# A two-layer graph network on one core: the statistics of a turn ahead of the copies on ScalarE, and folded weights spread over turns 0 to 2

## The chip, the core and the metric

The kernel runs on one core of a Trainium2 chip. The metric is the device time of one execution in microseconds (us); lower is better. The profile's engines are PE (TensorE, the matrix engine), DVE (VectorE), ACT (ScalarE), POOL (GpSimd) and SP (SyncE, which here only issues DMAs). Each engine works through its own queue in order, and waits for the others through semaphores.

## What is computed

The input is `x` (4096 nodes, 512 features) and an adjacency matrix `adj` (4096 x 4096, int32) with about 8 neighbours and the node itself in a row. Two layers are applied, each on a normalized and rectified copy of its input, and each adds its result to the input:

```python
def _L0_gnn_ref(x, adj, WQ, WK, WV, we, be):
    Q = (x @ WQ.T).reshape(n, HEADS, HEAD_DIM).transpose(1, 0, 2)
    ...
    energy = Q @ we.T + be
    attn = jnp.einsum('hqd,hkd->hqk', Q, K) * SCALING + energy
    attn = attn + jnp.where(adj > 0, 0.0, -jnp.inf)
    attn = jax.nn.softmax(attn, axis=-1)
    hard = (attn == jnp.max(attn, axis=-1, keepdims=True)).astype(jnp.float32) / HEADS
    out = jnp.einsum('hqk,hkd->hqd', hard, V)
    return out.transpose(1, 0, 2).reshape(n, EMBED)

def _L1_gnn_ref(x, adj, W_self, b_self, W_nb, b_nb, W_comb, b_comb):
    mask = (adj > 0).astype(x.dtype)
    deg = jnp.sum(mask, axis=1, keepdims=True)
    agg = mask @ x / jnp.maximum(deg, 1.0)
    self_f = x @ W_self + b_self
    nb_f = agg @ W_nb + b_nb
    combined = jnp.concatenate([self_f, nb_f], axis=-1)
    out = combined @ W_comb + b_comb
    return jax.nn.relu(out)

h = jnp.maximum(_layernorm(x, axis=-1), 0.0)
x = x + _L0_gnn_ref(h, adj, ...)
h = jnp.maximum(_layernorm(x, axis=-1), 0.0)
x = x + _L1_gnn_ref(h, adj, ...)
```

Layer 0 is an attention in which each of 8 heads takes the value of the one neighbour with the highest score. Layer 1 sums over the neighbours. `W_comb` is linear, so the kernel multiplies `W_self` and `W_nb` by its two halves once; that is what "fold" means below.

## The kernel before, in words

The work lies in `sparse_path`; `general_path` is compiled behind a flag and does not run on these inputs. There are 32 tiles of 128 nodes, and three phases.

**First phase (0 to about 330 us).** The adjacency is read and packed into words, every node's list of neighbours is found, keys and values are computed and written to `K_d` in DRAM, and the nodes are ranked by degree, so that the tiles are of falling degree. `CAPS` holds the number of list places for each tile (24 for tile 0, 5 for tile 31). What is left over of the value products (`late_v`) is done at the start of the next phase.

**Second phase (about 330 to 985 us).** A loop over turns `i` from -5 to 31 (line 1523). `turns` gives the tile of each turn: tiles 0 to 4 first, then alternately a tile of the lower half (turns 5, 7, 9, ... 27: "fused", whose key and value rows are fetched together) and one of the upper half (turns 6, 8, ... 26: "apart", whose eight winning values are fetched later, head by head), and three fused tiles last. The order of all instructions is written out by hand: each engine's queue has exactly the order of the Python code. One turn issues, in this order:

- on GpSimd, indirect DMAs: the key rows of this turn's tile (`key_gathers`), between them the values of an earlier tile (`value_gathers`), the row of the tile five turns ahead (`rows`), and near the turn's end the scatter of finished layer 1 rows into `G_d` (`scatter`, through `put_rows`, line 1119). The scatter reads `gs`. All gathers have line 1103.
- on ScalarE: `layer1_move` (line 1366, copies the neighbour product `pg` from PSUM to `gs`), `query_copy` (line 1173, `hqT`, for the tile two turns ahead), `layer1_copy` (line 1347, `hT1`), in fused turns the copy of the tile's own values `o` (line 1214), `layer1_stats` (lines 1302 to 1305), `query_norm` (lines 1159 to 1162, for the tile four turns ahead), copies of folded weights (line 1404), and later, after VectorE's reciprocal, `layer1_norm` (lines 1325 to 1329).
- on VectorE: `xo` (line 1288, the layer's sum for a tile of an earlier turn, first half of `layer1_stats`, with its store to `X1_d` on SP's queue), then `scores` (a product, line 1224, and a sum, line 1227, for each group of up to four list places). After the second group come `layer1_inverse` (line 1318, the reciprocal that needs the statistics) and `layer1_out` (line 1372, which reads `gs` and the self product `pr`). `winners` ends the turn: a few small instructions in an apart tile, and in a fused tile seven or eight `copy_predicated` (line 1260) as well.
- on TensorE: the query product of the next turn (line 628, `q`; PSUM holds two of them, so it waits until VectorE has read the last but one), folds, the layer 1 products (`pg` at line 628, `pr` at lines 1358 and 1360; both read `hT1`), the late value products in turns -2 to 0, and two sets of transposes (line 1138).

A dictionary `plan` says in which turn each tile has its steps. Statistics come in turns 3 to 31, one tile a turn up to turn 27 and two in turns 28 and 29; `hT1` and the layer 1 products from turn 5; the move and the scatter from turn 6.

**The folds.** `fold(k, i)` is four matmuls into one of three PSUM buffers and, for `i < 4`, a copy to a quarter of `wN` (k = 1) or `wS` (k = 0) on ScalarE. `i = 4` is the bias; its two products stay in PSUM until `fold_bias` adds them to `bb` on VectorE. `wS` takes the place of the value weights, which the late value products read up to turn 0. The fold's inputs lie in `room`, in which fused turns later put their gathered rows (from turn 5).

**Third phase (about 985 us to the end).** Rows of `G_d` are gathered and summed on VectorE, the widest eight tiles are summed as dense products on TensorE, and the result goes out.

The plan of folds and the part of the loop that is touched:

```python
between = {
    1: [(1, i) for i in range(NC)], 2: [(0, i) for i in range(NC)],
    3: [(1, NC), (0, NC)],
}
...
late(layer1_move, "move", i)
on(query_copy, i + 2)
late(layer1_copy, "layer1", i)
...
late(layer1_stats, "stats", i)
on(query_norm, i + 4)
on(query, i + 1)
for part in between.get(i, ()):
    fold(*part)
late(layer1, "layer1", i)
```

Of the kernel before, what the change touches and what calls it, by code (L numbers as in the profile page):

```python
# [20 lines left out]
NC = D // P  # L21
# [516 lines left out]
def sparse_path(  # L538
# [6 lines left out]
    KT = N // P  # L545
# [62 lines left out]
    def load_fold(k):  # L608
        nc.sync.dma_start(
            F[:, ds(2 * k * NC, NC), :],  # L610
            (wselfT, wnbT)[k].rearrange("(c p) f -> p c f", p=P),
        )
        nc.sync.dma_start(
            F[:, ds((2 * k + 1) * NC, NC), :],
            wcomb[ts(k, D), :].rearrange("(c p) f -> p c f", p=P),
        )
# [9 lines left out]
    def project(dst, h, w):  # L626
        for c in range(NC):
            nc.tensor.matmul(dst, h[:, c, :], w[:, c, :], start=(c == 0), stop=(c == NC - 1))  # L628

    with ExitStack() as pa:  # L630
# [195 lines left out]
        def values(t, ps):  # L826
            pv = ps.tile([P, D], F32, tag="pm", name="pv")
            project(pv, hT(t), ws["wv"])
            return pv

        def values_out(t, pv, pool, eng, vs=None):
            if vs is None:
                vs = pool.tile([P, D], F32, tag="gs", name="vs")

            nc.scalar.activation(vs, pv, AF.Copy, scale=1.0 / H)
            return eng.dma_start(K_d[ts(t, P), 0:D], vs)
# [93 lines left out]
        def on(step, t, *args):  # L930
            if 0 <= t < KT:
                step(t, *args)
# [159 lines left out]
    with ExitStack() as pb:  # L1092
# [9 lines left out]
        def gather(dst, src, idx, at=0):  # L1102
            last[0] = nc.gpsimd.indirect_dma_start(  # L1103
                out=dst, out_offset=None, in_=src,
                in_offset=bass.IndirectOffsetOnAxis(ap=idx, axis=0), element_offset=at,
            )
            if at:

                beyond.append(last[0])
                for w in written:  # L1110
                    tc.declare_no_dep(last[0].ins, w.ins, reason="other columns")
# [97 lines left out]
        def own_values(r):  # L1209

            s = st[r]
            s["o"] = xp.tile([P, D], F32, tag="o", name="o", bufs=3)
            if r in wide:
                nc.scalar.copy(s["o"], s["own"][:, 0:D])
            else:
                gather(s["o"], K_d[:, :], perm[:, r : r + 1])

        def scores(r, within):

            s = st[r]  # L1220
            sc = bp.tile([P, LIST, H], F32, tag="sc", name="sc", bufs=1)
            for kk, g0, g in s["kg"]:
                pr = bp.tile([P, GRP, D], F32, tag="pr", name="pr", bufs=1)
                nc.vector.tensor_tensor(  # L1224
                    pr[:, :g, :], s["q"].unsqueeze(1).to_broadcast([P, g, D]), kk, ALU.mult
                )
                nc.vector.tensor_reduce(  # L1227
                    sc[:, g0 : g0 + g, :],
                    pr[:, :g, :].rearrange("p g (h d) -> p g h d", h=H), AX.X, ALU.add,
                )  # L1230
                if g0:
                    within()
                    within = lambda: None
            s["sc"] = sc
# [148 lines left out]
        def load_bias():  # L1383
            for k in range(2):
                fb = bp.tile([P, D], F32, tag="own", name="fb")
                for c in range(NC):
                    nc.vector.tensor_copy(
                        fb[:, ts(c, P)], bcs[k][:, c : c + 1].to_broadcast([P, P])
                    )
                fbs.append(fb)  # L1390
# [4 lines left out]
        def fold(k, i):  # L1395

            pm = psm.tile([P, D], F32, tag="pm", name="pmw")
            if i < NC:
                left = F[:, ds(2 * k * NC, NC), ts(i, P)]
            else:  # L1400
                left = fbs[k].rearrange("p (c q) -> p c q", q=P)
            project(pm, left, F[:, ds((2 * k + 1) * NC, NC), :])
            if i < NC:
                nc.scalar.copy((wS, wN)[k][:, i, :], pm)
            else:
                biased.append(pm)

        def fold_bias():
            for pm in biased:
                nc.vector.tensor_tensor(bb, pm, bb, ALU.add)  # L1410

        between = {
            1: [(1, i) for i in range(NC)], 2: [(0, i) for i in range(NC)],
            3: [(1, NC), (0, NC)],
        }

        def dense_words():

            wg = gp.tile([P, DENSE, SEG], F32, tag="kg", name="wg")
            for r in range(DENSE):  # L1420
                gather(wg[:, r, :], W_d[:, :], perm[:, r : r + 1])
            return wg
# [50 lines left out]
        i = 0  # L1473
# [20 lines left out]
        def late(step, kind, i, *args):  # L1494

            out_ = []
            for r in turns:
                if plan[kind].get(r) == i:
                    out_ += step(r, *args) or []
            return out_  # L1500

        def tail_turn(r):

            k = tail.index(r)
            at = HALF_R + TAIL0 + k * D
            st[r]["hT1"] = room[:, at : at + D].rearrange("p (c q) -> p c q", q=P)
            nc.scalar.copy(st[r]["hT1"], st[r]["hnp"])

        def tail_product(r):
            s = st[r]  # L1510
            s["pg"] = psm.tile([P, D], F32, tag="pm", name="pg")
            project(s["pg"], s["hT1"], wN)

        def tail_move(r):
            s = st[r]
            s["gs"] = gsl[tail.index(r) // GRP][:, tail.index(r) % GRP]
            nc.scalar.copy(s["gs"], s["pg"])
            put_rows(G_d[:, :], r, s["gs"])
# [4 lines left out]
        for i in range(-5, KT):  # L1523


            if i == -3:
                load_fold(0)
            if i == 0:
                load_bias()
            if i == 1:  # L1530
                wS = wp.tile([P, NC, D], F32, tag="w_b", name="swS")
                wN = bp.tile([P, NC, D], F32, tag="swN", name="swN", bufs=1)
            a, b = on(key_gathers, i), late(value_gathers, "value", i)
            while a or b:
                for q, n in ((a, max(1, round(len(a) / max(1, len(b))))), (b, 1)):
                    for g in q[:n]:
                        gather(*g)
                    del q[:n]
            on(rows, i + 5)
            late(layer1_move, "move", i)  # L1540
            on(query_copy, i + 2)
            late(layer1_copy, "layer1", i)
            early = [r for r in tail if plan["turn"][r] == i - 1]
            for r in early:
                tail_turn(r)
            if i >= 0 and turns[i] in fused:
                own_values(turns[i])
            late(layer1_stats, "stats", i)
            on(query_norm, i + 4)
            on(query, i + 1)  # L1550
            for part in between.get(i, ()):
                fold(*part)
            late(layer1, "layer1", i)
            for r in early:
                tail_product(r)
            if i in (-2, -1, 0):
                n = 2
                for t in late_v[:n]:
                    w = values_out(t, values(t, psm), bp, nc.sync)
                    for g in beyond:  # L1560
                        tc.declare_no_dep(w.ins, g.ins, reason="other columns")
                    written.append(w)
                del late_v[:n]
            if i == max(between) + 1:
                fold_bias()

            def within():
                late(layer1_inverse, "stats", i)
                late(layer1_out, "move", i)

            if i >= 0:
                scores(turns[i], within)
            late(scatter, "move", i)
            if i == KT - 2:
                wg = dense_words()
                gsl = [gp.tile([P, GRP, D], F32, tag="kg", name="gs") for _ in range(2)]
            on(winners, i)
            late(layer1_norm, "stats", i)
            on(query_turn, i + 3)
            late(layer1_turn, "turn", i)  # L1580
            for r in early:
                tail_move(r)
# [161 lines left out]
def kernel(tc, *args):  # L1744
    left = sparse_path(tc, *args)
    with tc.If(left > 0):
        general_path(tc, *args)
# [40 lines left out]
```

## Time and profile before

| what | value |
|---|---|
| six executions, us | 1294.35, 1295.65, 1291.0, 1292.02, 1289.19, 1293.26 |
| their median, us | 1292.64 |
| the profiled execution, us | 1291.67 |
| its span, from first to last instruction, us | 1289.9 |
| PE busy | 1023.0 us (79%) |
| DVE busy | 989.1 us (77%) |
| POOL busy | 775.7 us (60%) |
| ACT busy | 427.6 us (33%) |
| granted TensorE clock, mean | 0.901 |

The busy shares are means over three unlike phases, so they don't say which engine ends which turn. The rows of single instructions do: each has its start, its duration, engine, line, what it writes and reads, how many were merged into the row, and in square brackets the time for which its engine stood idle before it, with what released it. "issue" stands for idle time in which the engine waited for nothing that the profile shows. An indirect DMA on POOL is busy only while GpSimd writes its descriptors; the data land some us later.

The page's slices (busy tenths of the engines in 40 equal parts of the span, 32 us each) show the second phase as slices 11 to 30:

```
DVE  5557777798289776889998889888782479788776
ACT  4778676731221222343434334443531000000000
POOL 2322323233477777777777777777554747777774
```

### The profile page before, as it was taken

What the parts mean: (1) busy time and instruction counts of PE and PEld (TensorE: products, weight loads), DVE (VectorE), ACT (ScalarE), POOL (GpSimd) and SP (SyncE); (2) the same over time, 40 slices, a digit from 0 to 9 for tenths busy, and PEclk for the clock granted to TensorE, in tenths of its full rate; (3) what the DMA queues carried; (4) which work ended last, traced back from release to release, by engine and by line L of the source; (5) the groups of instructions that cost most, each with busy time, mean ns of one, the idle gap of its engine ahead of it and who ended that gap; (6) DMA issues with size and microseconds to landing.
All of it is one profiled execution on the core that took longest, in us unless ns stands there. A gap on an engine that the chain in (4) does not pass through costs nothing.

```text
span 1289.9 us, 10765 instructions
## 1 busy us (share of the span) xinstructions
PE 1023.0 (79%) x2918; PEld 482.5 (37%) x2918; DVE 989.1 (77%) x1650; ACT 427.6 (33%) x880; POOL 775.7 (60%) x910
## 2 busy tenths in 40 slices
PE   5998998948779547757877887888789599999960
PEld 2555555524334223323333333333334244444420
DVE  5557777798289776889998889888782479788776
ACT  4778676731221222343434334443531000000000
POOL 2322323233477777777777777777554747777774
PEclk9999998978899868887889998988899799999985
DMA  9999999749585568888888888887754998888873
GB/s 358 420 420 421 418 420 328 260 147 373 192 255 166 155 187 237 272 272 257 264 264 258 252 249 262 264 246 240 276 179 130 314 347 273 282 272 272 283 248 122
DMA packets 109222, 350.09 MB, mean 271 GB/s; under 512 B 18064, under 2 KB 18064, under 8 KB 100960
## 3 DMA queue, kind: packets, MB, share of 16 engines
q0 software_dynamic: 63376, 208.23, 51.1%
q1 hardware_dynamic: 39552, 129.78, 26.0%
q10 hardware_dynamic: 6224, 11.31, 2.5%
q8 instruction: 25, 0.41, 0.1%
q14 instruction: 45, 0.37, 0.1%
HBM read 285.25 MB, written 68.19 MB: 274 GB/s over the span
## 4 chain that ended last, share of the span: by engine, by line
DMA 16%; POOL 15%; DVE 12%; issue 10%; PE 1%; ACT 1%; DVEq 0%; POOLq 0%
POOL room L1103 10%; DMA room<-G_d,sidx 6%; DMA room<-K_d,sidx 6%; DVE pr L1224 4%; DMA kg<-K_d,sidx 2%; POOL kg L1103 2%; DVE sc L1227 2%; DVE acc L1682 2%; POOL o L1103 2%; DVE o L1260 1%; PE pg L628 1%; DMA o<-K_d,perm 1%; DMA out_dram<-x,perm 1%; POOL out_dram L1119 1%; DVE x L1672 1%
## 5 line engine op out<-in xcount | busy, mean ns | idle before, releaser
L628 PE MATMUL q<-wq,hqT 128*128 128x512 f32 x256 | 160.4, 785 | 144.1 <-DVE pr L1224 144.1
L1660 PE MATMUL da<-gk,mk 128*128 128x512 f32 x512 | 222.5, 598 | 15.4 <-DMA gk<-G_d 15.4
L1103 POOL DMA_INDIRECT room<-G_d,sidx x174 | 179.2, 1030 | 57.7 <-issue 49.4
L1103 POOL DMA_INDIRECT kg<-K_d,sidx x177 | 170.9, 965 | 57.3 <-issue 45.3
L1227 DVE TENSOR_REDUCE sc<-pr 128x32 f32<-128x2048 f32 (+3 forms) x114 | 183.3, 1608 | 3.9
L1682 DVE TENSOR_REDUCE acc<-room 128x512 f32<-128x4096 f32 (+5 forms) x23 | 152.5, 6632 | 14.0 <-DMA room<-G_d,sidx 14.0
L1660 PEld LDWEIGHTS da<-gk,mk 128*128 128x128 f32 x512 | 98.2, 192 | 139.7 <-issue 139.5
L1103 POOL DMA_INDIRECT o<-K_d,vi x128 | 122.3, 955 | 39.0 <-issue 36.9
L628 PEld LDWEIGHTS q<-wq,hqT 128*128 128x128 f32 x256 | 61.8, 253 | 222.7 <-DVE pr L1224 125.7
L628 PE MATMUL pk<-wk,room 128*128 128x512 f32 x256 | 120.7, 616 | 4.2 <-ACT room L810 4.1
L628 PE MATMUL pv<-wv,room 128*128 128x512 f32 x256 | 116.3, 606 | 0.0
L1103 POOL DMA_INDIRECT room<-K_d,sidx x102 | 97.5, 955 | 31.1 <-issue 19.8
L1224 DVE TENSOR_TENSOR pr<-q,kg 128x2048 f32<-128x2048 f32 (+3 forms) x51 | 102.4, 2008 | 15.9 <-DMA kg<-K_d,sidx 14.6
L1224 DVE TENSOR_TENSOR pr<-q,room 128x2048 f32<-128x2048 f32 (+3 forms) x42 | 66.7, 1589 | 55.0 <-DMA room<-K_d,sidx 46.6
L1360 PE MATMUL pr<-swS,hT 128*128 128x512 f32 x216 | 99.9, 605 | 0.0
L628 PE MATMUL pg<-swN,hT 128*128 128x512 f32 x216 | 97.1, 592 | 0.0
L1302 ACT ACTIVATE hn<-xo 128x512 f32<-128x512 f32 x31 | 19.5, 629 | 196.5 <-DVE xo L1288 189.4
L749 ACT ACTIVATE mkt<-adjt,sgb 128x2048 bf16<-128x2048 int32 x37 | 74.2, 2005 | 12.3 <-POOL adjt L670 11.9
L824 POOL DMA_DIRECT2D K_d<-ks x32 | 18.7, 585 | 98.5 <-DVE ks L819 96.3
L1260 DVE COPY_PREDICATED o<-best,room 128x512 f32<-128x512 int32 x102 | 74.5, 730 | 3.5
L628 PEld LDWEIGHTS pv<-wv,room 128*128 128x128 f32 x256 | 49.8, 196 | 61.6 <-issue 61.4
L628 PEld LDWEIGHTS pk<-wk,room 128*128 128x128 f32 x256 | 48.3, 199 | 55.3 <-issue 48.9
(222 smaller groups left out, 1492.9 us busy)
## 6 DMA issues: line engine op xcount, KB each, us to landing
adjt<-adj_dram SPq DMA_DIRECT2D x37, 1024.0 KB, 12.2
room<-adj_dram SPq DMA_DIRECT2D x27, 1024.0 KB, 12.6
x<-X_d SPq DMA_DIRECT2D x32, 512.0 KB, 6.2
xt<-x_dram SPq DMA_DIRECT2D x32, 256.0 KB, 8.6
K_d<-ks POOLq DMA_DIRECT2D x32, 256.0 KB, 6.4
X_d<-xo SPq DMA_DIRECT2D x32, 256.0 KB, 4.2
X_d<-own SPq DMA_DIRECT2D x32, 256.0 KB, 4.8
gk<-G_d ACTq DMA_DIRECT2D x16, 512.0 KB, 5.8
```

The source lines that it names most:

```text
L628: nc.tensor.matmul(dst, h[:, c, :], w[:, c, :], start=(c == 0), stop=(c == NC - 1))
L749: nc.scalar.activation(mk, st[t]["adj"][j], AF.Sigmoid, bias=sgb, scale=400.0, accum_out=degs[:, t, j : j + 1],)
L824: nc.gpsimd.dma_start(K_d[ts(t, P), D : 2 * D], ks)
L1103: last[0] = nc.gpsimd.indirect_dma_start(out=dst, out_offset=None, in_=src, in_offset=bass.IndirectOffsetOnAxis(ap=idx, axis=0), element_o ...
L1119: new = nc.gpsimd.indirect_dma_start(out=dst, out_offset=bass.IndirectOffsetOnAxis(ap=perm[:, r : r + 1], axis=0), in_=src, in_offset=None,)
L1224: nc.vector.tensor_tensor(pr[:, :g, :], s["q"].unsqueeze(1).to_broadcast([P, g, D]), kk, ALU.mult)
L1227: nc.vector.tensor_reduce(sc[:, g0 : g0 + g, :], pr[:, :g, :].rearrange("p g (h d) -> p g h d", h=H), AX.X, ALU.add,)
L1260: nc.vector.copy_predicated(s["o"].rearrange("p (h d) -> p h d", h=H), best[:, k, :].bitcast(I32).unsqueeze(2).to_broadcast([P, H, HD]), b ...
L1302: nc.scalar.activation(junk, xo, AF.Copy, scale=-1.0 / D, accum_out=q[:, 0:1])
L1360: nc.tensor.matmul(pr, s["hT1"][:, c, :], wS[:, c, :], start=False, stop=(c == NC - 1))
L1660: nc.tensor.matmul(dacc[r], masks[s][:, h, r, :], keys[s][:, h, :], start=(s == 0 and h == 0), stop=(s == NPL - 1 and h == 1),)
L1682: nc.vector.tensor_reduce(acc, g[:, 0:n, :].rearrange("p n f -> p f n"), AX.X, ALU.add)
```

## The change

Three things are moved; no instruction is added or taken away.

1. In turns before 28 (`KT - 4`), `layer1_stats` (with its `xo`) is issued ahead of `layer1_move`, `query_copy`, `layer1_copy` and the own values, rather than behind them. From turn 28 on it stays where it was.
2. The eight folds of the weights are issued in turns 0, 1 and 2, as three, three and two, rather than four in turn 1 and four in turn 2. The two bias products stay in turn 3. `wN` is therefore set up in turn 0, `wS` still in turn 1.
3. `fold_bias`, in turn 4, is issued right behind the folds, ahead of the layer 1 products.

```diff
         between = {
-            1: [(1, i) for i in range(NC)], 2: [(0, i) for i in range(NC)],
+            0: [(1, 0), (1, 1), (1, 2)], 1: [(1, 3), (0, 0), (0, 1)], 2: [(0, 2), (0, 3)],
             3: [(1, NC), (0, NC)],
         }
...
             if i == 1:
                 wS = wp.tile([P, NC, D], F32, tag="w_b", name="swS")
+            if i == 0:
+                wS = None
                 wN = bp.tile([P, NC, D], F32, tag="swN", name="swN", bufs=1)
...
             on(rows, i + 5)
+            if i < KT - 4:
+                late(layer1_stats, "stats", i)
             late(layer1_move, "move", i)
             on(query_copy, i + 2)
             late(layer1_copy, "layer1", i)
...
                 own_values(turns[i])
-            late(layer1_stats, "stats", i)
+            if i >= KT - 4:
+                late(layer1_stats, "stats", i)
             on(query_norm, i + 4)
             on(query, i + 1)
             for part in between.get(i, ()):
                 fold(*part)
+            if i == max(between) + 1:
+                fold_bias()
             late(layer1, "layer1", i)
...
-            if i == max(between) + 1:
-                fold_bias()
```

## The prediction

> **What bounds the kernel now.** I first looked at the slices of the page, to see which stretch the edits touch, then at the busy time of each engine in that stretch, then at what GpSimd and VectorE wait for there, and last at the order of time around single turns. The edits touch turns 0 to 27, which in the trace run from 360 to 900 us. The table of stretches (busy us and instructions of each engine) has this for most of it:
>
> ```profile
> core 0: us, PE busy (x) PEld busy (x) DVE busy (x) ACT busy (x) POOL busy (x), PEclk, DMA share, GB/s
> ...
> 396.00:934.00 538.00, 402.45 (x973) 176.43 (x972) 456.53 (x552) 191.62 (x495) 402.96 (x419) 0.87 0.79 243
> ```
>
> GpSimd looks free a quarter of the time, and is not. Its rows there, nearly all gathers, take 0.95 us with 0.30 us before each, whatever released them. 419 rows of 1.25 us are 524 of the 538 us, and most of the rest is one idle time of 8.47 us at the window's end (934.79): up to there no hole is left. VectorE (457 us) does wait; its waits in the same window:
>
> ```profile
> DVE pr L1224 <- DMA room<-K_d,sidx: 41.4, 16, 5.8
> DVE pr L1224 <- DMA kg<-K_d,sidx: 14.6, 8, 4.0
> DVE pr L1224 <- issue: 8.3, 2, 5.8
> DVE q L1318 <- ACT q L1304: 4.2, 1, 4.2
> ```
>
> So in turns 3 to 28 VectorE is late because gathers land late, and they land late because GpSimd issues one after another. The second thing to see is how little the wait that the change aims at weighs: the reciprocal (line 1318) waits for ScalarE's statistics once, 4.2 us at 929.87, in turn 29, and turns from 28 on keep their order.
>
> Now the place of the copies, at the border of turns 9 and 10 (start, us, engine, line). ScalarE:
>
> ```profile
> 577.29 0.59 ACT L1347 COPY hT<-tr 128x512 f32<-128x512 f32 x1
> 591.08 0.63 ACT L1302 ACTIVATE hn<-xo 128x512 f32<-128x512 f32 x1 [13.19 <-DVE xo L1288]
> ...
> 592.88 0.28 ACT L1305 ACTIVATE q<-q,c 128x1 f32<-128x1 f32 x1
> 593.07 0.19 ACT L1159 CAST sidx<-km 128x24 int32<-128x24 f32 x1
> ```
>
> GpSimd at the same time:
>
> ```profile
> 590.18 0.95 POOL L1103 DMA_INDIRECT room<-K_d,perm  x1 [0.31 <-issue]
> 591.43 0.99 POOL L1119 DMA_INDIRECT G_d<-gs,perm  x1 [0.30 <-DMA kg<-K_d,sidx]
> 592.73 0.96 POOL L1103 DMA_INDIRECT room<-K_d,sidx  x1 [0.31 <-DVE sc L1227]
> ```
>
> The three copies of turn 10 were over by 578, and ScalarE then stood 13.19 us in front of the statistics, because `xo` follows VectorE's winners of turn 9. The scatter of turn 10 (line 1119) reads `gs`, the first of those copies, and sits in GpSimd's queue ahead of all gathers of turn 11.
>
> **The change, part by part.** (1) *Statistics first, turns 3 to 27.* The instructions are the same; `xo` and its store on SP's queue keep their place among VectorE's. What is new is a wait: behind the statistics on ScalarE now stand the move to `gs`, the query copy, `hT1` and, in odd turns, the own values. Who waits for each:
>
> - The gain: no wait of the reciprocal lies in these turns, so 0. ScalarE was idle before each of these statistics (25 waits for `xo`, 185.7 us): the copies never held them up.
> - `hT1` is wanted by TensorE's layer 1 products. It comes at the statistics' start S + 1.99 (591.08 to 593.07) and three copies at a pitch of 0.5: S + 3.6. In turn 10 that is 594.7, while the query product ended at 586.2: TensorE gets a hole of 8.5 us. The products' results are read in the next turn: `gs` at the next S + 2, the self product by line 1372 at about the next S + 6, and S to S is 14 to 25 us. With 8.4 us of products (3.60 + 1.12 + 3.70) and 1.0 of transposes TensorE is done at S + 13, and the query product after it, 3.6 us, is wanted a whole turn later. Cost 0; if the hole makes the products cold, see below, still 0.
> - The query copy serves a product issued a turn later, the own values (0.64) winners some 10 us later: 0.
> - `gs`, wanted by the scatter: here the cover is thin. The scatter can't start before S + 1.99, plus the copy's 0.56, plus 0.28 from its end to GpSimd's start (in turn 30 the copy ends at 934.51, the scatter that waits for it starts at 934.79): S + 2.83. I set that against the scatter's present start in each turn. Odd turns have 2.6 to 8.3 us to spare. Even turns, from 6 to 26: -0.13 (512.86 against 510.16 + 2.83), 1.35, **-2.48** (591.43 against 591.08 + 2.83), 0.81, 1.44, 0.78, 0.78, -0.10 (771.33 against 768.60 + 2.83), 3.30, 2.04, 2.04.
>
> In three turns the scatter becomes late, by 0.13 + 2.48 + 0.10 = 2.7 us, with every gather behind it. GpSimd has no hole to make that good in, and VectorE waits for gathers in each odd turn (turn 13: 0.26 and 2.28), so the whole rest shifts: after turn 10 the scatter and S move together, and the later margins stay. At 934.79 GpSimd does idle, 8.47 us, but for a copy that itself hangs on VectorE; no cover there either.
>
> Bounds: the latency that I read once, and the landing of the last gather before each border (5.0 us from issue to use in turn 7, 6.3 in turn 9), move all margins. One us better leaves 1.5 us (turn 10 alone). One us worse gives 1.13 + 3.48 + 0.19 + 0.22 + 0.22 + 1.10 = 6.3. A lost margin costs while a gained one gives nothing, so I take a quarter us to the worse side: 0.38 + 2.73 + 0.35 = **3.5 us**.
>
> (2) *Folds from turn 0.* The same 32 products and eight copies as before, in turns 0, 1, 2 as 3, 3, 2. TensorE's two fold blocks of 13.90 us (393.61, 411.74) hid behind VectorE's scores, which run without a break from 360.68 to 431: gain 0. In turn 0 three folds (3 x 3.43 = 10.3 us) go ahead of the two last value products, into a hole of 8.57 us before 387.26: the next query product ends near 393 instead of 393.6 and is wanted at 411.43. The last `vs` copy moves from 378.3 to 388.6, its store from 378.9 to 389.2; with the 4.5 us that such stores take it lands at 393.7, ahead of the first value gather on GpSimd (398.46). With the 9.4 us of the slowest store on that line it would be 398.6: 0 to 0.15, I take 0. The weights were in place by 324 (issued 304 to 316, landing 8 to 13).
> (3) *`fold_bias` ahead of layer 1.* In turn 4 VectorE has nothing in between, and no layer 1 product is planned before turn 5: 0.
>
> Sum: +3.5 us. The profiled execution took 1291.67 us (span 1289.9 and 1.77 around it), so 1295.2; it ran 0.97 below the median of the six runs, so on the median 1292.64 + 3.5 = **1296.1**.
>
> A rule that speaks against the change stands in the Trainium skill, "TensorE: Matmul & The Clock Gate", part 1 (the HAM clock gate): after an idle window of about 3.4 us TensorE falls to half its clock, and needs about as long to come back. The rows go the same way, with a smaller loss: the query product took 6.17 us after an idle 10.24 us (562.05), 3.60 without (618.29). By the rows a cold start costs the products 2.6 us; by the rule, taken as cold throughout (an estimate), 8.4 more. Either ends before the next turn's copy wants it, so the sum is the same by both.
>
> **Rivals.**
> - *The scatter is late in nearly every even turn.* If `gs` came 2 us later than S + 2.83 (more waits between the statistics and the move), eight even turns would lose: 2.13 + 0.65 + 4.48 + 1.19 + 0.56 + 1.22 + 1.22 + 2.10 = 13.5 us, 1306.2. For it: five margins lie between 0.78 and 1.44. Against: the copies follow one another at 0.5 us in the trace, and the move waits for a product long done. It decides from about 1 us on.
> - *The delay is absorbed.* In turn 11 the first gathers land over 2 us early (last issued at 600.28, used at 608.72), so VectorE feels little there. If queued transfers then landed as much sooner as they were issued later, nothing is left: 1292.6. Against: GpSimd issues without a hole until 934, so a lost us is not won back.
> - *Faster.* One place could give something: GpSimd's two idle moments for VectorE's buffers in turns 0 and 2 (1.34 at 364.69, 2.66 at 395.95). If earlier folds ended both, 4.0 us: 1288.6. Against: both hang on VectorE's unbroken scores, which start when the first query product ends at 360.5, before any fold.
>
> **How the numbers follow.** A measurement of this kernel tells about 0.3% (3.9 us) from no change. The forecast (1.5 to 6.3 us) has 0.60, of which 0.35 lies under 3.9 and 0.25 above; many late scatters 0.20; absorbed 0.12; faster 0.08. That makes slower 0.25 + 0.20 = 0.45, same 0.35 + 0.12 = 0.47, faster 0.08. The forecast's own range is 1294.1 to 1298.9. The stated range takes in the absorbed case less the runs' scatter of 2 us, and most of the late-scatter rival: 1290.5 to 1304.
>
> **What would show it.** In the new profile ScalarE's order is statistics, move, copies; GpSimd shows waits for `gs` at line 1119 in turn 10 of about 2.5 us and small ones in turns 6 and 20, and none in odd turns; line 1318 waits no less than before; TensorE idles between query and layer 1 products in even turns; the folds start near 371 and the time at which VectorE begins turn 3 is unmoved. I am wrong if line 1119 waits in most even turns, if VectorE waits for TensorE or ScalarE in turns 3 to 27, or if GpSimd's pitch of 1.25 us changes.

## The result, and the profile after

The changed kernel takes 1298.48 us (median of 19 runs, 1294.45 to 1300.42) against 1293.13 us for the kernel before (40 runs, 1288.06 to 1296.64): a ratio of 1.0043, with a 95% interval of 1.0033 to 1.0053, or 5.6 us more (4.3 to 6.9). Here and below, ratios compare only executions in the faster of the two states in which a kernel can run. By the prediction's bar of 0.3% (3.9 us) the change is slower. The profiled execution spans 1294.5 us (before 1289.9).

The time went where GpSimd issues. The table of stretches has this for the same window as before:

```profile
core 0: us, PE busy (x) PEld busy (x) DVE busy (x) ACT busy (x) POOL busy (x), PEclk, DMA share, GB/s
396.00:934.00 538.00, 397.68 (x946) 171.50 (x944) 454.08 (x543) 183.93 (x476) 402.44 (x419) 0.85 0.79 241
```

GpSimd has the same 419 instructions; VectorE gets nine fewer done in the window (543 against 552). The pitch of 1.25 us is unchanged, so the loss must be holes between GpSimd's instructions. The order of time in turn 10, GpSimd first (start, length, instruction, idle time before it and what ended that):

```profile
591.71 0.95 POOL L1103 DMA_INDIRECT room<-K_d,perm  x1 [0.30 <-issue]
595.95 0.99 POOL L1119 DMA_INDIRECT G_d<-gs,perm  x1 [3.28 <-ACT gs L1366]
597.24 0.96 POOL L1103 DMA_INDIRECT room<-K_d,sidx  x1 [0.30 <-issue]
```

and ScalarE in the same microseconds:

```profile
593.12 0.63 ACT L1302 ACTIVATE hn<-xo 128x512 f32<-128x512 f32 x1 [16.02 <-DVE xo L1288]
...
594.92 0.28 ACT L1305 ACTIVATE q<-q,c 128x1 f32<-128x1 f32 x1
595.11 0.56 ACT L1366 COPY gs<-pg 128x512 f32<-128x512 f32 x1
595.57 0.58 ACT L1173 COPY hqT<-tr 128x512 f32<-128x512 f32 x1
596.05 0.59 ACT L1347 COPY hT<-tr 128x512 f32<-128x512 f32 x1
```

ScalarE idles 16.02 us in front of the statistics with a finished product behind them. The move ends at 595.67 and the scatter starts at 595.95, exactly 2.83 us after the statistics began at 593.12. It comes 2.98 us later than its queue would have let it, and the gather behind it follows at the usual 0.30: nothing is caught up.

The other holes of the stretch, as time above the usual 0.30 us: turn 6 has 0.21, turn 20 has 0.15, both at line 1119 and both foreseen. Two were not foreseen. The scatter of turn 26 starts 0.66 late although `gs` had been finished 1.75 us before. And behind the scatter of turn 18 the first gather of turn 19 stood for no reason that the trace names:

```profile
740.34 0.99 POOL L1119 DMA_INDIRECT G_d<-gs,perm  x1 [0.30 <-ACT gs L1366]
743.30 0.97 POOL L1103 DMA_INDIRECT room<-K_d,sidx  x1 [1.98 <-issue]
```

That is 1.68 more. The sum is 0.21 + 2.98 + 1.68 + 0.15 + 0.66 = 5.7 us, and the measured loss, between the medians of many executions, is 5.6. The delay can also be followed from turn to turn: the scatter lies 1.52 us behind its time in the kernel before in turn 9, 4.52 in turn 10, 4.32 in turn 18, 6.32 in turn 19 (the gathers between are the hole shown above) and 6.61 in turn 27. The first 1.7 of these are older than the change: in this execution the first indirect gather of the second phase came at 338.80 instead of 337.11, ahead of every edit. So the two profiled executions by themselves agree less closely: from just ahead of turn 6 to turn 29 the lag grows from 1.54 to 6.82, by 5.3 us; at turn 30 it is 5.71, since turn 30's own wait is 0.9 shorter (7.55 for 8.47); and the spans differ by 4.6, of which 1.7 are older than the change. Why part of it came back in the third phase, the runs do not show.

VectorE waits at the same line for the same things as before (line, what it waits for: us, times, longest), and for no other engine. Only the waits without a named releaser grew, from 8.3 to 13.4; the reciprocal's wait in turn 29 now lies behind the window's end:

```profile
DVE pr L1224 <- DMA room<-K_d,sidx: 41.0, 16, 5.8
DVE pr L1224 <- DMA kg<-K_d,sidx: 13.9, 6, 3.9
DVE pr L1224 <- issue: 13.4, 3, 5.2
```

### The profile page after: what moved, and what is told of

Read it like the earlier page. It is cut to its first block, busy times and chain, and to the rows that moved or that the text cites. A ratio compares the mean times of both kernels' runs of the same rounds, so it can differ in the third digit from the quotient of the medians.

```text
span 1294.5 us, 10776 instructions
## 1 busy us (share of the span) xinstructions
PE 1027.8 (79%) x2918; PEld 481.8 (37%) x2918; DVE 989.3 (76%) x1650; ACT 426.9 (33%) x880; POOL 774.0 (60%) x910
## 4 chain that ended last, share of the span: by engine, by line
DVE 27%; DMA 22%; POOL 20%; issue 15%; PE 12%; ACT 3%; DVEq 0%; POOLq 0%; SPq 0%; ACTq 0%
POOL room L1103 10%; DMA room<-G_d,sidx 7%; DVE pr L1224 7%; DMA room<-K_d,sidx 5%; DVE sc L1227 4%; POOL kg L1103 4%; POOL o L1103 4%; PE pk L628 4%; DMA kg<-K_d,sidx 4%; DMA adjt<-adj_dram 3%; PE pv L628 3%; DVE o L1260 3%; PE pw L768 2%; DVE acc L1687 2%; PE pg L628 1%
## 5 line engine op out<-in xcount | busy, mean ns | idle before, releaser
L628 PE MATMUL pg<-swN,hT 128*128 128x512 f32 x216 | 128.9, 752 | 89.1 <-ACT hT L1347 89.0
L628 PE MATMUL q<-wq,hqT 128*128 128x512 f32 x256 | 133.0, 668 | 53.5 <-DVE pr L1224 53.5
L1687 DVE TENSOR_REDUCE acc<-room 128x512 f32<-128x4096 f32 (+5 forms) x23 | 152.6, 6634 | 13.6 <-DMA room<-G_d,sidx 13.5
L628 PEld LDWEIGHTS pg<-swN,hT 128*128 128x128 f32 x216 | 50.5, 244 | 165.5 <-ACT hT L1347 106.8
L628 PEld LDWEIGHTS q<-wq,hqT 128*128 128x128 f32 x256 | 52.5, 216 | 111.5 <-issue 78.2
L824 POOL DMA_DIRECT2D K_d<-ks x32 | 18.7, 585 | 98.2 <-DVE ks L819 96.0
```

Source lines behind the costliest of these rows:

```text
L824: nc.gpsimd.dma_start(K_d[ts(t, P), D : 2 * D], ks)
L1687: nc.vector.tensor_reduce(acc, g[:, 0:n, :].rearrange("p n f -> p f n"), AX.X, ALU.add)
```

## Experiments

The theory is the prediction's: the move to `gs`, put behind a wait for VectorE, makes the scatter late, and GpSimd can't make that good. The rivals are that TensorE's late and cold layer 1 products cost the time, or that the folds do, or that it is the statistics' earlier place as such.

**One half at a time.** The first kernel moves the statistics and leaves the folds as before; the second has the folds and the bias as in the changed kernel and leaves the statistics in their old place.

```diff
 # e1_stats_only, against the kernel before
             on(rows, i + 5)
+            if i < KT - 4:
+                late(layer1_stats, "stats", i)
             late(layer1_move, "move", i)
...
-            late(layer1_stats, "stats", i)
+            if i >= KT - 4:
+                late(layer1_stats, "stats", i)
 # e2_folds_only, against the changed kernel: these lines undone
```

> Only the statistics are moved ahead of the copies; folds and bias as before. Theory (the scatter waits for gs on GpSimd's queue): the whole loss of the change, ratio 1.004, with waits at line 1119 of about 3 us in turn 10 and under 1 us in turns 6 and 20. Rival (TensorE's products run late and cold behind the copy of hT1): also 1.004, with about 89 us of TensorE waiting for hT1. Rival (the folds cost something): 1.000 to 1.002.

> Only the folds and the bias sum are moved; the statistics stay behind the copies. Theory: 1.000, since TensorE has a hole in turn 0 and the stores of the last values land before the first value gather; no wait at line 1119 up to turn 28. Rival (the folds cost something): 1.002 to 1.004.

Statistics alone: 1.0035 (1.0021 to 1.0050), 4.5 us. Folds alone: 1.0006 (0.9992 to 1.0020). The two halves add up to the whole (0.35 + 0.06 against 0.43%). With the statistics alone GpSimd waits at line 1119 for 0.52 us in turn 6 and 3.00 in turn 10, and 2.07 at turn 19's first gather: above 0.30 that is 4.7 us. With the folds alone no scatter waits up to turn 28; one gather stands 1.02 us, at 606.55 (the tail kernel below has 0.88 there, the others nothing), and the time is within the noise. The interval leaves up to 0.2% for the folds; the next kernel, which has them too, is no slower either.

**TensorE or GpSimd.** In the changed kernel the layer 1 products do wait for `hT1`, 89.0 us in 19 turns, and the neighbour products take 752 ns each instead of 592. Two kernels separate that from the scatter. One puts the move alone ahead of the statistics again, so that `hT1` stays late and `gs` is early; the other takes the kernel before and puts the move alone behind the statistics.

```diff
 # e3_move_first, against the changed kernel
             on(rows, i + 5)
+            late(layer1_move, "move", i)
             if i < KT - 4:
                 late(layer1_stats, "stats", i)
-            late(layer1_move, "move", i)
 # e4_move_last, against the kernel before
-            late(layer1_move, "move", i)
+            if i >= KT - 4:
+                late(layer1_move, "move", i)
...
             late(layer1_stats, "stats", i)
+            if i < KT - 4:
+                late(layer1_move, "move", i)
```

> The changed kernel with the move to gs put ahead of the statistics again; query copy, hT1 and own values stay behind them. Theory (scatter): 1.000, no wait at line 1119 up to turn 28, while TensorE still waits some 89 us for hT1 and its first layer 1 products still take about 750 ns each. Rival (TensorE late and cold): still 1.004.

> The kernel before with the move to gs alone put behind the statistics; query copy, hT1, own values and folds stay as before. Theory (scatter): the whole loss, 1.004, waits at line 1119 as in the changed kernel, while TensorE does not wait for hT1. Rival (TensorE late and cold): 1.000.

With the move first the loss is gone: 1.0005 (0.9986 to 1.0023). Yet TensorE's largest wait from 360 to 945 us is nearly that of the changed kernel, and its products stay as slow (749 ns):

```profile
PE pg L628 <- ACT hT L1347: 84.2, 20, 9.3
```

With only the move behind the statistics the loss is there: 1.0049 (1.0031 to 1.0068), 6.3 us, though no product waits for `hT1` and the neighbour products take 592 ns. TensorE is not untouched there: the self products wait 27.5 us for the move and take 691 ns instead of 605. But that is less than the kernel with the move first bears at no cost. So 84 us of waits and products a quarter slower cost nothing that the runs can tell, and one copy of 0.56 us in the wrong place costs all of it. GpSimd's rows of this last kernel, the scatter of turn 10 and the first gather of turn 19:

```profile
595.26 0.99 POOL L1119 DMA_INDIRECT G_d<-gs,perm  x1 [3.08 <-ACT smeta L1160]
...
742.59 0.97 POOL L1103 DMA_INDIRECT room<-K_d,sidx  x1 [2.06 <-issue]
```

The holes of turn 19 and turn 26 are here again (2.06 and 1.00, with the usual 0.30 in them). In the first row `smeta` is named as the releaser because it ended last before the start, at 595.20; the move ended at 594.98, and 0.28 later, at 595.26, the scatter starts, as it does in turn 10 of the changed kernel. `smeta` is read by other instructions.

**More of it.** If lateness of the move is the cause, a still later move costs more, by the margins in the prediction. This kernel puts it behind `query_norm` as well, some 1 us later.

```diff
 # e11_move_later, against the kernel before
-            late(layer1_move, "move", i)
+            if i >= KT - 4:
+                late(layer1_move, "move", i)
...
             on(query_norm, i + 4)
+            if i < KT - 4:
+                late(layer1_move, "move", i)
```

> The kernel of e5_move_later a third time, in the hope of a chip on which the kernel before takes 1293 us. There: theory (scatter), by the margins of the profile before, 4 us slower than e4_move_last, ratio 1.008 to the kernel before; rival (a fixed cost of any move behind the statistics): 1.005. On a chip like that of e8_move_later (1423 us) again 1.038.

1306.37 us, 1.0097 (1.0077 to 1.0117), or 12.5 us. GpSimd's rows:

```profile
515.61 1.02 POOL L1119 DMA_INDIRECT G_d<-gs,perm  x1 [1.53 <-ACT gs L1366]
...
556.99 0.99 POOL L1119 DMA_INDIRECT G_d<-gs,perm  x1 [1.33 <-ACT gs L1366]
...
598.73 0.99 POOL L1119 DMA_INDIRECT G_d<-gs,perm  x1 [4.28 <-ACT gs L1366]
...
708.40 0.99 POOL L1119 DMA_INDIRECT G_d<-gs,perm  x1 [1.24 <-ACT gs L1366]
...
744.79 0.99 POOL L1119 DMA_INDIRECT G_d<-gs,perm  x1 [1.36 <-ACT gs L1366]
...
747.85 0.97 POOL L1103 DMA_INDIRECT room<-K_d,sidx  x1 [2.07 <-DVE own L1372]
...
782.78 0.99 POOL L1119 DMA_INDIRECT G_d<-gs,perm  x1 [1.30 <-ACT gs L1366]
...
884.41 0.99 POOL L1119 DMA_INDIRECT G_d<-gs,perm  x1 [1.38 <-issue]
```

Each less 0.30: 1.23 + 1.03 + 3.98 + 0.94 + 1.06 + 1.77 + 1.00 + 1.08 = 12.1 us for the 12.5 measured. The direction and the law hold; the size that was expected from the margins did not. Turns 6, 10 and 20 give 6.2 for the 5.9 that the margins said, but turns 8, 16, 18, 19 and 26 add another 5.9 where half a microsecond was expected. Of these, 3.0 are scatters (turns 8, 16, 18) whose margins had shrunk: the margins of the prediction are those of one execution, and they move by about a microsecond from one kernel to the next. The other 2.9 are the holes of turns 19 and 26 again.

**A way back.** If a wait at the head of GpSimd's queue is lost time, the longest one, the 8.47 us ahead of the scatter of turn 30 in the kernel before, should be worth something too. In turn 30 this kernel issues the scatter behind the gathers of the dense words, which wait for nothing:

```diff
 # e12_tail, against the kernel before
-            late(scatter, "move", i)
+            if i != KT - 2:
+                late(scatter, "move", i)
             if i == KT - 2:
...
                 gsl = [gp.tile([P, GRP, D], F32, tag="kg", name="gs") for _ in range(2)]
+                late(scatter, "move", i)
```

> The kernel of e7_tail a third time. Where the kernel before takes 1293 us: theory (an idle GpSimd ahead of gathers is lost time) 0.996 to 0.998, GpSimd's wait of 8.5 us in turn 30 gone and VectorE's wait of 5.1 us at the start of turn 31 with it; rival (the last turns hang on TensorE and ScalarE) 1.000.

1286.86 us, 0.9948 (0.9930 to 0.9967): 6.7 us faster than the kernel before, and the fastest of all. That is more than the 3 to 5 us expected; where the rest comes from is not shown. The scatter finds `gs` ready, and the gathers of turn 31 start at 941.42 instead of 946.18. In this execution the scatter of turn 29 lay 3.6 us behind its time in the kernel before, so the gain in turn 30 is 8.4 us:

```profile
938.87 0.95 POOL L1103 DMA_INDIRECT wg<-W_d,perm  x1 [0.30 <-issue]
940.12 1.00 POOL L1119 DMA_INDIRECT G_d<-gs,perm  x1 [0.31 <-issue]
941.42 0.97 POOL L1103 DMA_INDIRECT room<-K_d,sidx  x1 [0.30 <-issue]
```

VectorE's first group of gathered rows in the next tile is then there in time. In the kernel before:

```profile
957.26 2.29 DVE L1224 TENSOR_TENSOR pr<-q,room 128x2048 f32<-128x2048 f32 x1 [5.11 <-DMA room<-K_d,sidx]
```

and with the scatter moved:

```profile
953.60 0.69 DVE L1227 TENSOR_REDUCE sc<-pr 128x8 f32<-128x512 f32 x1
954.32 2.29 DVE L1224 TENSOR_TENSOR pr<-q,room 128x2048 f32<-128x2048 f32 x1
```

**On two other chips.** The last two kernels, and a third that gives the changed kernel's scatters one turn more, had been run before on two chips on which the kernel before took 1418.25 and 1423.48 us:

```diff
 # e6_scatter_next and e9_scatter_next, against the changed kernel
+            if 0 < i <= KT - 4:
+                late(scatter, "move", i - 1)
             on(rows, i + 5)
...
-            late(scatter, "move", i)
+            if i >= KT - 4:
+                late(scatter, "move", i)
 # e5_move_later and e8_move_later are e11_move_later; e7_tail and e10_tail are e12_tail
```

> A larger dose: the kernel before with the move to gs alone put behind the statistics and behind the query's norm as well, so that gs is ready about 1.07 us later than in e4_move_last. Theory (scatter): with the margins of the profile before, turns 6, 10, 12, 16, 18 and 20 are late by 1.20, 3.55, 0.26, 0.29, 0.29 and 1.17 us, 6.8 in all against 2.7 by the same sum for the smaller dose: 4 us slower than e4_move_last, ratio 1.008 to the kernel before. Rival (a fixed cost of any move behind the statistics): as e4_move_last, 1.005.

> The changed kernel with the scatter of a turn put behind the key and value gathers of the next turn (turns before 28); ScalarE's order and the folds as changed. Theory (scatter): gs is ready long before, GpSimd has no wait at line 1119 up to turn 28, 1.000. Rival (ScalarE's or TensorE's order itself costs): 1.004.

> The same reading used for a gain on the kernel before: in turn 30 the scatter, before which GpSimd idles 8.5 us for gs, is put behind the eight gathers of the dense words (10 us of work that waits for nothing). Theory (an idle GpSimd ahead of gathers is lost time): the gathers of turn 31 start 8 us earlier, VectorE's wait of 5.1 us for them at the start of turn 31 goes, 3 to 5 us faster, ratio 0.996 to 0.998. Rival (the last turns hang on TensorE and ScalarE): 1.000.

> The kernel of e5_move_later again, on another chip: there TensorE itself issued its products with gaps of up to 9 us, and the kernel before took 1418 us, so the comparison does not bear on the margins of the profile. As before: theory (scatter) 4 us slower than e4_move_last, ratio 1.008 to the kernel before; rival (a fixed cost of any move behind the statistics): 1.005.

> The kernel of e6_scatter_next again, for the same reason. Theory (scatter): no wait at line 1119 up to turn 28, 1.000. Rival (ScalarE's or TensorE's order itself costs): 1.004.

> The kernel of e7_tail again, for the same reason. Theory (an idle GpSimd ahead of gathers is lost time): 0.996 to 0.998. Rival (the last turns hang on TensorE and ScalarE): 1.000.

| kernel | first chip (1418 us before) | second chip (1423 us before) | usual chip (1293 us before) |
|---|---|---|---|
| move later (e5, e8, e11) | 1.0375 (1.0344 to 1.0407) | 1.0385 (1.0341 to 1.0429) | 1.0097 (1.0077 to 1.0117) |
| scatter a turn later (e6, e9) | 1.0374 (1.0341 to 1.0407) | 1.0320 (1.0231 to 1.0408) | not run |
| tail (e7, e10, e12) | 0.9943 (0.9904 to 0.9982) | 0.9999 (0.9965 to 1.0033) | 0.9948 (0.9930 to 0.9967) |

On these chips TensorE is late too. The waits of TensorE in the tail kernel, on the second chip, from 360 to 1100 us:

```profile
PE q L628 <- issue: 130.4, 68, 14.6
PE pmw L628 <- issue: 30.8, 8, 10.5
PE pg L628 <- ACT hT L1347: 21.2, 9, 9.1
```

TensorE stands 130.4 us ahead of query products with nothing named that it waits for, which no trace of a usual chip shows. With its products so late, the cover that the prediction gave `hT1` (a whole turn) is gone: with the scatter a turn later products wait 174.9 us for `hT1` there, and VectorE 70.6 us at line 1372, 18.7 at the longest. Neither expectation came about for the first two kernels, whose loss is over 3% there, and of the tail's two runs one fits the theory (0.9943) and one the rival (0.9999). So these six runs decide nothing between the theories. That a scatter issued one turn later would take the loss away on a usual chip was not tried.

## Why the prediction was right

**The mechanism** was the one named: the move to `gs` queues behind statistics that wait for `xo`, the scatter waits for `gs` at the head of GpSimd's queue, and the rest of the phase shifts. Moving that one copy forward takes the loss away, and moving it alone makes it. The forecast of this mechanism had a chance of 0.60, and only part of it lay above the bar of 3.9 us: "same" stood at 0.47 and "slower" at 0.45, so the prediction had the cause and the range, and left open on which side of the bar the time would fall.

**The term that was mis-sized** is the sum of the scatter's lateness, 3.5 us taken against 5.6 measured, inside its bounds of 1.5 to 6.3. The three turns named in it, 10, 6 and 20, were 2.73, 0.38 and 0.35 and came out at 2.98, 0.21 and 0.15: 3.3 us together. The other 2.3 us are turn 19's first gather (1.68) and turn 26's scatter (0.66). The step behind it is the latency of 0.28 us from the copy's end to GpSimd's start, read once and taken for every turn. It held at each scatter that waited in turns 6, 10 and 20, and not at these two places, as the next paragraph shows. That the later margins stay, as the prediction has it, did not hold either: turn 18's went from 0.78 to 0.10. That the whole still fell inside the bounds is partly luck: they allow the latency 1 us more, and at these two places it is longer than that.

**Two places with a longer way.** Where the scatter waits for the move, it starts 0.27 to 0.29 us after the move's end. The scatter of turn 26 and the first gather of turn 19 start later than that, each at a distance of its own from the move. In the changed kernel the moves of turns 18 and 26 and the scatter of turn 26 are these:

```profile
739.40 0.56 ACT L1366 COPY gs<-pg 128x512 f32<-128x512 f32 x1
...
876.09 0.56 ACT L1366 COPY gs<-pg 128x512 f32<-128x512 f32 x1
...
878.40 0.99 POOL L1119 DMA_INDIRECT G_d<-gs,perm  x1 [0.96 <-ACT smeta L1160]
```

From the end of the move (start plus 0.56) to GpSimd's start, in us:

| kernel | turn 18's move to turn 19's first gather | turn 26's move to its scatter |
|---|---|---|
| changed | 743.30 - 739.96 = 3.34 | 878.40 - 876.65 = 1.75 |
| statistics alone | 741.48 - 738.15 = 3.33 | 2.32, not late |
| move behind the statistics | 742.59 - 739.25 = 3.34 | 877.46 - 875.71 = 1.75 |
| move later | 747.85 - 744.51 = 3.34 | 884.41 - 882.65 = 1.76 |
| move later, on the two other chips | 3.34, 3.34 | 1.76, 1.75 |
| tail, on the two other chips | 3.33, 3.34 | 1.75, 1.76 |

In the one kernel in which turn 26's scatter is not late, GpSimd comes to it only 2.32 us after the move. In the kernels without these two holes (before, folds alone, move first, and the tail on the usual chip) the move ends 10 us or more ahead of these scatters. So both holes hang on the end of the move like the others, whatever ScalarE does before or after it; the releasers that the rows name there (`smeta`, `hq`, none, `own`) differ from kernel to kernel and are not the cause. Why GpSimd needs 1.5 and 1.8 us more at these two places, and nowhere else behind a move of turns 6 to 29, the runs do not show.

**The rival of many late scatters** did not come about as long as the move follows the statistics at once, and nearly did with 1 us more: 12.1 us of holes in the kernel with the move later, against the 13.5 worked out. The prediction put the point from which it decides at about 1 us, and with 1 us the run has eight holes, two of them at the places just named.

**What was put at nothing** was nothing. The 8.5 us hole ahead of the products in turn 10 is there (8.42 us; 8.5 at the longest, in turn 20), with smaller ones in eight odd turns too, and 84 us of them cost 0.05% with zero inside the interval. The folds begin at 372.75, three of them in 10.46 us, and gave 0.06% with zero inside. Turn 3 begins its statistics at 432.58 against 431.07, 1.5 us later, which is the offset of 1.7 from before the phase and no more. The reciprocal waits once, 3.6 us instead of 4.2; the prediction had said no less, but this is in turn 29, where the order is as before.

**The cold products** did come, but their cost was moved rather than added. The costliest groups of the page after have these lines (busy us and mean ns of one, idle time ahead):

```profile
L628 PE MATMUL pg<-swN,hT 128*128 128x512 f32 x216 | 128.9, 752 | 89.1 <-ACT hT L1347 89.0
L628 PE MATMUL q<-wq,hqT 128*128 128x512 f32 x256 | 133.0, 668 | 53.5 <-DVE pr L1224 53.5
```

Before, the neighbour products took 97.1 us (592 ns each, no idle time ahead) and the query products 160.4 (785 ns each, 144.1 us of idle time ahead). TensorE's idle time now lies ahead of other products, and the slow start goes with it: 31.8 us more for the one, 27.4 less for the other. The prediction counted the loss (2.6 us a turn by the rows) and overlooked the gain. In turn 10 the neighbour products took 6.62 us instead of 3.60 after their hole of 8.42 us, at a granted clock of 0.53 (596.60 to 603.00), and the self products behind them took 3.70 as before. The half clock of the Trainium skill ("TensorE: Matmul & The Clock Gate", part 1) is there in the rows; the 8.4 us by which the prediction priced it came from taking all products as cold throughout, which they were not.

## What to carry to other kernels

When an instruction is put behind a wait, follow its result to the queue in which the reader stands, and ask whether that queue has holes: here TensorE had them and lost nothing from 84 us of waits, and GpSimd had none, so its holes added up to the loss. In an issue queue without holes, put work that waits for nothing ahead of the instruction that waits; one scatter placed so gave 0.5% on the usual chip. Margins under a microsecond read from one execution are good for the sign and not for the count of turns that lose, and a latency read at one place need not hold at the next.

## What the runs showed of the hardware

A VectorE addition with both inputs in SBUF holds up a gather that starts inside it. `xo` (line 1288) ran from 663.90 to 664.57 in the changed kernel:

```profile
663.90 0.67 DVE L1288 TENSOR_TENSOR xo<-km,o 128x512 f32<-128x512 f32 x1
```

and GpSimd beside it:

```profile
662.75 0.95 POOL L1103 DMA_INDIRECT kg<-K_d,sidx  x1 [0.30 <-DMA kg<-K_d,sidx]
664.01 1.39 POOL L1103 DMA_INDIRECT kg<-K_d,sidx  x1 [0.30 <-issue]
665.70 0.95 POOL L1103 DMA_INDIRECT kg<-K_d,sidx  x1 [0.30 <-issue]
```

The gather that starts at 664.01 has 0.56 us of `xo` ahead of it and takes 1.39, the others 0.95. In the traces of the usual chips such a gather lasts what is left of `xo` plus 0.81 to 0.85 us, where at least 0.15 us are left and `xo` began at least 0.05 us before it: 1.03 with 0.20 left, 1.43 with 0.60 left (both in the kernel before). The products of line 1224, which read one input from PSUM, and the sums do not do it (at most 0.98). Five to ten gathers of a run are hit, 1.4 to 2.9 us in all, no more in the changed kernel (7, 2.2 us) than before (9, 2.8 us), so it explains none of the difference. The Trainium skill, "SBUF — State Buffer", "Who interferes with whom", has the rule: a VectorE instruction with two SBUF inputs contends with a GpSimd instruction that reads SBUF. The rows agree, and show it for the issue of an indirect DMA, whose indices lie in SBUF; the same section's inference that such an addition leaves the writing of descriptors alone does not fit these rows.

The other surprise is the chips: the same kernel took 1293 us on the usual ones and 1418 to 1423 on two, where TensorE idles with no releaser named (130.4 us ahead of query products in the one case above), and an edit worth 1.0% on the usual chip was worth 3.8% there.
